# Attention's probabilities turned by VectorE in 32x32 squares instead of by TensorE

## The chip, the cores and the metric

The kernel runs on one core of one Trainium2 chip. TensorE multiplies matrices and can transpose a 128x128 block by a product with an identity matrix, writing to PSUM. VectorE, ScalarE and GpSimd (POOL) work beside it, each with a queue that it works off in order. SyncE (SP) issues the transfers (DMA), also in order. The metric is device time in microseconds, lower is better.

## The reference

A block of a gated cross-attention model on `x` of 8 batches x 512 tokens x 512 columns, all in float32.

```
a  = layernorm(x)
Q, K, V = a @ Wq.T + bq,  ctx @ Wk.T + bk,  ctx @ Wv.T + bv      # 16 heads of 32
P  = softmax(Q K^T / sqrt(32))                                    # per batch and head, 512 x 512
x  = x + tanh(g_xattn) * ((P V) @ Wo.T + bo)
x  = x + tanh(g_ffn) * mixture_of_experts(layernorm(x))           # 8 experts, top 2, capacity 615
```

## The kernel before, in words

The first half of the kernel is attention, the second the experts; the change lies in the first alone.

Attention is cut into 128 **units** (b, c, qc): a batch, a group of four heads (`QH` = 4) and a block of 128 queries. The main loop runs over them in that order, so four units share a (b, c) pair and sixteen a batch. The order of every engine's instructions is the order in which the Python code emits them (`tc.manual_schedule()`); buffers of the pools (`bufs`) and semaphores decide when each can start.

What happens to one unit:

- `scores(u)`: four products of 32 rows (one per head) put 128 queries x 512 keys per head into two PSUM tiles of two banks (`ps_s`, four banks, one unit at a time). VectorE takes the negative row maxima (`nm`, L349, two instructions).
- `soften(u)`: ScalarE takes four exponentials (L356), one per head, into `pr`, and adds up each row (`sums`).
- `turn_heads(u, heads, evict)`: the weights have to be turned, because the product with V sums over keys and so needs keys in the partitions. `turned` (L235) makes four TensorE transposes per head, sixteen per unit, into the ring `ps_t` (two banks). Heads 0 and 1 are copied out by ScalarE (`on_act`, L407), heads 2 and 3 by VectorE (`on_dve`, L410), to `p_t`, one tile per head for the four query blocks of a (b, c) pair.
- `weighted(b, c)`: once the fourth unit of a pair is turned, sixteen products (four key blocks x four heads, 512 columns, L388) give the weighted values `po`. VectorE takes the reciprocals of the sums, POOL spreads them to 32 columns per head (`wide`).
- `divide(b, c, ...)`: four TensorE transposes (L401) turn the reciprocals into `pt_r`, ScalarE copies them (`over`, L403) and VectorE multiplies into `o_t` (L404).

One iteration n of the loop emits, in this order: loads for later (`loads`, SP), the scores of unit n+1, small work on layer norms and the router (`pre`), the weighted values of the last pair if n starts a new one, the turning of heads 0 and 1 of unit n, the exponentials of unit n+1, one projection (`main`: q, k, v or o in turn, L299), `divide`, further small work (`more`: layer norm rows turned on TensorE, router products L276, `add_bo` on POOL), and the turning of heads 2 and 3 of unit n.

A float32 product counts as two matrix instructions in the profile, a transpose as one. Lines in the profile: L251 and L268 copy turned layer norm rows, L218 to L228 are the layer norm on VectorE, L319 and L328 take the v and o projections out of PSUM, L308 and L313 the q and k projections.

The experts' stage already uses the two steps that the change brings into attention: `lay_in` and `lay_out` (L810, L841) move 32-row quarters of a tile inside SBUF by transfers, and `turn_laid` and `lay_out` (L820, L833) transpose 32x32 squares on VectorE.

Of the kernel before, what the change touches and what calls it, by code (L numbers as in the profile page):

```python
# [17 lines left out]
P = 128  # L18
# [3 lines left out]
DC = D // P  # L22
# [22 lines left out]
def gated_block(ctx: ExitStack, tc: tile.TileContext, a: dict, out: bass.AP):  # L45
# [125 lines left out]


    with ExitStack() as at:
        wts = at.enter_context(tc.tile_pool(name="wts", bufs=1))
# [3 lines left out]
        ps_s = at.enter_context(tc.tile_pool(name="ps_s", bufs=2, space=PSUM))  # L178
        ps_t = at.enter_context(tc.tile_pool(name="ps_t", bufs=2, space=PSUM))
        ps_p = at.enter_context(tc.tile_pool(name="ps_p", bufs=1, space=PSUM))  # L180
        ps_o = at.enter_context(tc.tile_pool(name="ps_o", bufs=1, space=PSUM))

# [87 lines left out]
        def route(b):  # L270

            xt = rows_n.pop((3, b))
            pl = ps_o.tile([P, S], F32, tag="po", name="pl")[:, :P]
            for c in range(DC):
                for j in range(TT):
                    nc.tensor.matmul(  # L276
                        pl[j * HD : (j + 1) * HD, :],
                        lhsT=wr[:, c, :],
                        rhs=xt[:, c, j, :],
                        start=(c == 0),  # L280
                        stop=(c == DC - 1),
                    )
            lt = small.tile([P, P], F32, name="lt", bufs=1)
            nc.scalar.activation(lt, pl, AF.Identity, bias=br_c)
            rows_n[4, b] = lt

        def route_turn(b):
            pl = ps_o.tile([P, S], F32, tag="po", name="pl_t")[:, :P]
            nc.tensor.transpose(pl, rows_n.pop((4, b)), ident)
            nc.vector.tensor_copy(  # L290
                logits[:, b * TT : (b + 1) * TT, :], pl.rearrange("p (j e) -> p j e", j=TT)[:, :, :E]
            )
# [12 lines left out]
        def proj_q(b, c, ps=None):  # L305
            ps = group(lambda ic: w["q"][:, ic, cols(c)], lambda ic: xn_t[b][:, ic, :], ps)
            q_t[b, c] = acts.tile([P, S], F32, tag="q_t", name="q_t")
            nc.scalar.activation(q_t[b, c], ps, AF.Identity, bias=bq[:, c : c + 1], scale=SCALE)  # L308

        def proj_k(b, c, ps=None):  # L310
            ps = group(lambda ic: w["k"][:, ic, cols(c)], lambda ic: ctx_t[b][:, ic, :], ps)
            k_t[b, c] = acts.tile([P, S], F32, tag="k_t", name="k_t")
            nc.scalar.activation(k_t[b, c], ps, AF.Identity, bias=bk[:, c : c + 1])  # L313

# [14 lines left out]

        p_sb, p_t, sums, recips = {}, {}, {}, {}  # L330

# [20 lines left out]
        def soften(u, ps, nm):  # L352
            b, c, qc = u
            pr = probs.tile([P, QH, S], F32, tag="pr", name="pr")
            for i in range(QH):
                nc.scalar.activation(  # L356
                    pr[:, i, :],
                    ps[i // 2][:, i % 2, :],
                    AF.Exp,
                    bias=nm[:, i : i + 1],  # L360
                    accum_out=sums[b, c][:, qc, i : i + 1],
                )
            p_sb[u] = pr

        def turn_heads(u, heads, evict):
            b, c, qc = u
            if qc == 0 and heads[0] == 0:
                p_t[b, c] = [
                    probs.tile([P, TT, S], F32, tag=f"p_t{i}", name=f"p_t{i}", bufs=1) for i in range(QH)
                ]  # L370
            for i in heads:
                pt = turned(p_sb[u][:, i, :])
                evict(p_t[b, c][i][:, :, cols(qc)], pt)

        def weighted(b, c):

            if c == 0:
                o_t[b] = acts.tile([P, DC, S], F32, tag="o_t", name=f"o_t{b}")
            rc = small.tile([P, TT, QH], F32, name="rc", bufs=2)
            nc.vector.reciprocal(rc, sums.pop((b, c)))  # L380
            wide = small.tile([P, TT, QH, HD], F32, name="wide", bufs=1)
            nc.gpsimd.tensor_copy(wide, rc.unsqueeze(3).to_broadcast([P, TT, QH, HD]))
            po = ps_o.tile([P, S], F32, tag="po", name="po")
            pts = p_t.pop((b, c))
            for kc in range(TT):
                for i in range(QH):
                    h = QH * c + i
                    nc.tensor.matmul(  # L388
                        po[i * HD : (i + 1) * HD, :],
                        lhsT=v_s[b][:, kc, h * HD : (h + 1) * HD],  # L390
                        rhs=pts[i][:, kc, :],
                        start=(kc == 0),
                        stop=(kc == TT - 1),
                    )
            return po, wide

        def divide(b, c, po, wide):

            pt = ps_t.tile([P, TT, P], F32, tag="pt", name="pt_r")
            for qc in range(TT):  # L400
                nc.tensor.transpose(pt[:, qc, :], wide[:, qc, :, :].rearrange("p h d -> p (h d)"), ident)  # L401
            over = probs.tile([P, S], F32, tag="over", name="over", bufs=1)
            nc.scalar.copy(over, pt.rearrange("p c q -> p (c q)"))  # L403
            nc.vector.tensor_tensor(o_t[b][:, c, :], po, over, ALU.mult)  # L404

        def on_act(dst, src):
            nc.scalar.copy(dst, src)  # L407

        def on_dve(dst, src):
            nc.vector.tensor_copy(dst, src)  # L410

# [42 lines left out]
        for j, t in enumerate((2, 3, 6, 7)):  # L454
            put_ln2(B - 2, (11, 13, 14, 15), B - 1, j, t)

        def loads(b, c, qc):
            if qc == 2 and c == 2 and b + 2 < B:
                load_ctx(b + 2)
            if qc == 0:  # L460
# [7 lines left out]
                if c == DC - 1:  # L468
                    load_x(b, 0, 2)
                    if b == B - 2:  # L470
                        load_x(b, 1, 2)
                elif b == B - 1 and c == 0:
# [5 lines left out]
        with tc.manual_schedule():  # L478
# [44 lines left out]
            nc.gpsimd.tensor_scalar(bo_b, bo_b, tg_x, None, ALU.mult)  # L523
            for n, u in enumerate(units):
                b, c, qc = u
                loads(b, c, qc)
                nxt = units[n + 1] if n + 1 < len(units) else None
                if nxt:
                    ps, nm = scores(nxt)
                for f, *args in pre.pop(n, ()):  # L530
                    f(*args)
                if n and qc == 0:
                    out_of = units[n - 1][:2]
                    po_wide = weighted(*out_of)
                turn_heads(u, (0, 1), on_act)
                if nxt:
                    soften(nxt, ps, nm)
                for f, *args in main.pop(n, ()):
                    f(*args)
                if n and qc == 0:  # L540
                    divide(*out_of, *po_wide)
                for f, *args in more.pop(n, ()):
                    f(*args)
                turn_heads(u, (2, 3), on_dve)
                p_sb.pop(u)

            last = B - 1
            for j in range(1, TT):
                load_x(last, j, 2)
            for j in range(TT):  # L550
                add_bo(last, j)
            divide(last, DC - 1, *weighted(last, DC - 1))
            choose_largest(small, last - 1, 0)
            choose_largest(small, last - 1, 1)
            choose_gates(last - 1)
            assert not pre and not main and not more
# [680 lines left out]
```

## Time and profile before

| | us |
|---|---|
| median of 3 runs | 2106.46 (2105.45 to 2106.7) |
| the profiled execution, its own time | 2106.64 |
| its span, first to last instruction | 2104.5 |

Of the span TensorE's matmuls are busy 95%, its weight loads 59%, VectorE 62%, ScalarE 40%, POOL 29%. Attention runs from the first loads to about 1050 us, the choice of tokens for the experts to about 1120 us, the experts from there to the end.

How the rows are read: the page gives the span in 40 slices, with a digit for the tenths of each slice in which an engine is busy, and a digit for the clock granted to TensorE. A row of windows gives busy microseconds of each engine in one stretch, with instruction counts in brackets. A row of groups names line, engine, operation, tile written and tiles read, shapes and count; then busy time, the mean of one in ns, and the engine's idle time just before, with what ended it.

### The profile page before, as it was taken

What the parts mean: (1) busy time and instruction counts of PE and PEld (TensorE: products, weight loads), DVE (VectorE), ACT (ScalarE), POOL (GpSimd) and SP (SyncE); (2) the same over time, 40 slices, a digit from 0 to 9 for tenths busy, and PEclk for the clock granted to TensorE, in tenths of its full rate; (3) what the DMA queues carried; (4) which work ended last, traced back from release to release, by engine and by line L of the source; (5) the groups of instructions that cost most, each with busy time, mean ns of one, the idle gap of its engine ahead of it and who ended that gap; (6) DMA issues with size and microseconds to landing.
All of it is one profiled execution on the core that took longest, in us unless ns stands there. A gap on an engine that the chain in (4) does not pass through costs nothing.

```text
span 2104.5 us, 27762 instructions
## 1 busy us (share of the span) xinstructions
PE 1994.6 (95%) x9808; PEld 1238.7 (59%) x9808; DVE 1297.9 (62%) x2694; ACT 836.1 (40%) x2014; POOL 604.6 (29%) x800
## 2 busy tenths in 40 slices
PE   8999999999999999999848999999999999999997
PEld 3445555555555555555426676777777777777775
DVE  4566566566665666656566768676767767663540
ACT  3556555555555555555502214041322304032231
POOL 1001101001100101010014374564536455464533
PEclk9999999999999999999969999999999999999998
DMA  6010111102010110100042244544453444535331
GB/s 220 1 56 16 51 41 45 41 21 69 28 56 31 31 65 21 32 31 36 26 122 66 70 117 96 148 110 130 96 134 87 108 120 106 151 84 139 92 74 25
DMA packets 216938, 157.46 MB, mean 75 GB/s; under 512 B 17568, under 2 KB 186208, under 8 KB 216800
## 3 DMA queue, kind: packets, MB, share of 16 engines
q1 hardware_dynamic: 207968, 134.81, 22.1%
q0 software_dynamic: 8832, 20.88, 5.3%
q8 instruction: 78, 1.28, 0.2%
q14 instruction: 60, 0.49, 0.1%
HBM read 107.75 MB, written 29.77 MB: 65 GB/s over the span
## 4 chain that ended last, share of the span: by engine, by line
PE 81%; DVE 6%; ACT 5%; issue 3%; DMA 2%; SPq 2%; POOL 0%; POOLq 0%; ACTq 0%; DVEq 0%
PE ps L900 36%; PE pj L299 20%; PE pt L235 11%; PE s L340 7%; PE po L388 5%; DMA w<-in_W 2%; SPq L841 1%; DVE ht L884 1%; ACT q_t L308 1%; ACT xn_t L268 1%; ACT xn_t L251 1%; ACT over L403 1%; PE pj_o L299 1%; DVE mask L667 1%; ACT h L924 1%
## 5 line engine op out<-in xcount | busy, mean ns | idle before, releaser
L356 ACT ACTIVATE pr<-s,nm 128x512 f32<-128x512 f32 x512 | 347.1, 704 | 2.5 <-DVE nm L349 2.5
L235 PEld LDWEIGHTS pt<-ident,pr 128*128 128x128 f32 x2048 | 224.8, 141 | 175.0 <-DVE p_t L410 76.6
L235 PE MATMUL pt<-ident,pr 128*128 128x128 f32 x2048 | 293.0, 279 | 34.1 <-ACT over L403 13.9
L349 DVE TENSOR_REDUCE nm<-s 128x2 f32<-128x1024 f32 x256 | 301.4, 1218 | 38.2 <-PE s L340 37.4
L407 ACT COPY p_t<-pt 128x512 f32<-128x512 f32 x256 | 137.5, 589 | 408.1 <-PE pt L235 408.1
L222 POOL TENSOR_TENSOR rstd<-rstd,nhalf 128x1 f32<-128x1 f32 x64 | 37.2, 582 | 688.6 <-DVE rstd L221 688.6
L900 PE MATMUL ps<-xg_t,w 128*128 128x308 f32 x768 | 220.1, 423 | 0.5 <-ACT u L953 0.5
L410 DVE COPY p_t<-pt 128x512 f32<-128x512 f32 x256 | 169.7, 686 | 70.6 <-PE pt L235 68.3
L900 PE MATMUL ps<-h,w 128*128 128x308 f32 x768 | 207.5, 425 | 0.0
L900 PEld LDWEIGHTS ps<-xg_t,w 128*128 128x128 f32 x768 | 145.8, 190 | 53.9 <-ACT u L953 1.0
L900 PEld LDWEIGHTS ps<-h,w 128*128 128x128 f32 x768 | 143.7, 190 | 52.6 <-issue 3.1
L340 PE MATMUL s<-k_t,q_t 32*128 32x512 f32 x1024 | 152.2, 646 | 2.9 <-ACT pr L356 2.0
L900 PE MATMUL ps<-tg,s1w 128*128 128x308 f32 x512 | 145.4, 426 | 9.3 <-ACT p1s L928 9.3
L404 DVE TENSOR_TENSOR o_t<-po,over 128x512 f32<-128x512 f32 x32 | 22.1, 691 | 191.6 <-ACT over L403 191.6
L900 PE MATMUL ps<-ht,s2w 128*128 128x308 f32 x512 | 137.9, 426 | 0.0
L924 ACT ACTIVATE h<-c,b 128x308 f32<-128x308 f32 x192 | 101.2, 549 | 74.4 <-DVE c L963 72.7
L900 PEld LDWEIGHTS ps<-tg,s1w 128*128 128x128 f32 x512 | 94.9, 190 | 53.0 <-issue 20.4
L299 PE MATMUL pj<-ctx_t,wk 128*128 128x512 f32 x256 | 117.3, 602 | 7.0 <-DMA ctx_t<-in_ctx_t 7.0
L388 PE MATMUL po<-p_t,v_s 128*32 128x512 f32 x1024 | 119.4, 599 | 0.0
L900 PEld LDWEIGHTS ps<-ht,s2w 128*128 128x128 f32 x512 | 95.5, 190 | 34.8 <-issue 1.8
L356 ACT ACTIVATION_READ_ACCUMULATOR pr<-s,nm 128x1 f32 x512 | 113.9, 222 | 0.0
L299 PE MATMUL pj<-xn_t,wq 128*128 128x512 f32 x248 | 111.6, 592 | 0.0
(192 smaller groups left out, 2960.9 us busy)
## 6 DMA issues: line engine op xcount, KB each, us to landing
w<-in_W SPq DMA_DIRECT2D x128, 256.0 KB, 3.3
w<-in_W SPq DMA_DIRECT2D x64, 512.0 KB, 3.8
x<-in_x SPq DMA_DIRECT2D x64, 256.0 KB, 4.3
laid<-xg SPq DMA_DIRECT2D x140, 64.0 KB, 2.6
out_x<-x SPq DMA_DIRECT2D x32, 256.0 KB, 2.0
xn_rows<-xn SPq DMA_DIRECT2D x32, 256.0 KB, 2.0
ctx_t<-in_ctx_t SPq DMA_DIRECT2D x7, 1024.0 KB
eo<-laid SPq DMA_DIRECT2D x112, 64.0 KB, 2.1
```

Of the source, the lines that this page charges most:

```text
L222: nc.gpsimd.tensor_tensor(rstd, rstd, nhalf, ALU.pow)
L235: nc.tensor.transpose(pt[:, c, :], src[:, c * P : (c + 1) * P], ident)
L299: nc.tensor.matmul(ps, lhsT=lhs(ic), rhs=rhs(ic), start=(ic == 0), stop=(ic == DC - 1))
L340: nc.tensor.matmul(ps[i // 2][:, i % 2, :], lhsT=q_t[b, c][r, cols(qc)], rhs=k_t[b, c][r, :], start=True, stop=True,)
L349: nc.vector.tensor_reduce(nm[:, 2 * i : 2 * i + 2], ps[i], AX.X, ALU.max, negate=True)
L356: nc.scalar.activation(pr[:, i, :], ps[i // 2][:, i % 2, :], AF.Exp, bias=nm[:, i : i + 1], accum_out=sums[b, c][:, qc, i : i + 1],)
L388: nc.tensor.matmul(po[i * HD : (i + 1) * HD, :], lhsT=v_s[b][:, kc, h * HD : (h + 1) * HD], rhs=pts[i][:, kc, :], start=(kc == 0), stop=(k ...
L404: nc.vector.tensor_tensor(o_t[b][:, c, :], po, over, ALU.mult)
L407: nc.scalar.copy(dst, src)
L410: nc.vector.tensor_copy(dst, src)
L900: nc.tensor.matmul(ps, lhsT=lhs[k], rhs=rhs[k], start=(k == 0 and not onto), stop=(k == n - 1), skip_group_check=onto,)
L924: nc.scalar.activation(hh[q, i], src, AF.Silu, bias=b1[:, j : j + 1])
```

## The change

The weights of a unit are no longer turned on TensorE. A 128x128 transpose is split into two steps: rows are moved so that 32x32 squares stand where they must, and VectorE transposes the squares.

- `soften` writes `pr` with the keys in four groups (`[P, DC, QH, P]`) and then issues four transfers on SP, one per group: group g of all 128 rows (256 KB) goes to partitions 32g to 32g+31 of a new tile `laid_p`, four rows of `pr` behind one another in each partition.
- `turn_heads` is now one VectorE square transpose per head, 128x512, from `laid_p` to `p_t`; the ScalarE and VectorE copies out of PSUM are gone.
- So that this comes out in the right order, the q projection stores its columns and the k projection its keys in a permuted order, and the copy `over` undoes the order of the queries (strided access patterns on ScalarE).
- `weighted` now runs per unit, sixteen products of 128 columns instead of sixteen of 512 per pair, two units after the unit's scores block: iteration n emits heads 0 and 1 of unit n-1 turned, scores of n+1, the weighted values of unit n-2, exponentials and transfers of n+1, and heads 2 and 3 of unit n-1. The loop has two more iterations.
- `over_sums` holds the reciprocals and `wide`, after the pair's fourth unit; `divide` follows in the same iteration, now the second of the next pair.
- PSUM: the ring `ps_t` has one bank instead of two, `ps_o` two instead of one; the router's results use `ps_t`.
- Loads: the context of batch b+2 comes in four transfers instead of one; the last batch's x is loaded at its last head group and `add_bo` for it runs in its last four iterations; the choice of the last but one batch (`choose_largest`, `choose_gates`) stands before the last weighted values.

```diff
-        ps_t = at.enter_context(tc.tile_pool(name="ps_t", bufs=2, space=PSUM))
+        ps_t = at.enter_context(tc.tile_pool(name="ps_t", bufs=1, space=PSUM))
-        ps_o = at.enter_context(tc.tile_pool(name="ps_o", bufs=1, space=PSUM))
+        ps_o = at.enter_context(tc.tile_pool(name="ps_o", bufs=2, space=PSUM))
...
-            nc.scalar.activation(q_t[b, c], ps, AF.Identity, bias=bq[:, c : c + 1], scale=SCALE)
+            nc.scalar.activation(
+                q_t[b, c].rearrange("p (t j q) -> p t q j", t=TT, q=DC),
+                ps.rearrange("p (t q j) -> p t q j", t=TT, q=DC),
+                AF.Identity, bias=bq[:, c : c + 1], scale=SCALE,
+            )
...
-            nc.scalar.activation(k_t[b, c], ps, AF.Identity, bias=bk[:, c : c + 1])
+            nc.scalar.activation(
+                k_t[b, c].rearrange("p (g c i) -> p c g i", g=DC, c=DC),
+                ps.rearrange("p (c g i) -> p c g i", g=DC, c=DC),
+                AF.Identity, bias=bk[:, c : c + 1],
+            )
...
         def soften(u, ps, nm):
             b, c, qc = u
-            pr = probs.tile([P, QH, S], F32, tag="pr", name="pr")
+            pr = probs.tile([P, DC, QH, P], F32, tag="pr", name="pr")
             for i in range(QH):
                 nc.scalar.activation(
-                    pr[:, i, :],
-                    ps[i // 2][:, i % 2, :],
+                    pr[:, :, i, :],
+                    ps[i // 2][:, i % 2, :].rearrange("p (g k) -> p g k", g=DC),
                     AF.Exp,
...
+            laid_p[u] = probs.tile([P, DC, QH, P], F32, tag="laid_p", name="laid_p")
+            for g in range(DC):
+                nc.sync.dma_start(
+                    out=laid_p[u][g * BL : (g + 1) * BL].rearrange("p q h k -> p (q h k)"),
+                    in_=pr[:, g].rearrange("p h k -> p (h k)"),
+                )
...
-            for i in heads:
-                pt = turned(p_sb[u][:, i, :])
-                evict(p_t[b, c][i][:, :, cols(qc)], pt)
+        def turn_heads(u, heads):
+            if heads[0] == 0:
+                p_t[u] = probs.tile([P, QH, TT, P], F32, tag="p_t", name="p_t")
+            for i in heads:
+                nc.vector.transpose(
+                    p_t[u][:, i].rearrange("p c (q j) -> p q c j", q=DC),
+                    laid_p[u][:, :, i].rearrange("p q (c i) -> p q c i", c=DC),
+                )
+
+        def weighted(u):
+            b, c, qc = u
+            if qc == 0:
+                values[b, c] = ps_o.tile([P, S], F32, tag="po", name="po")
+            pt = p_t.pop(u)
+            for kc in range(TT):
+                for i in range(QH):
+                    h = QH * c + i
+                    nc.tensor.matmul(
+                        values[b, c][i * HD : (i + 1) * HD, cols(qc)],
+                        lhsT=v_s[b][:, kc, h * HD : (h + 1) * HD],
+                        rhs=pt[:, i, kc, :],
+                        start=(kc == 0),
+                        stop=(kc == TT - 1),
+                    )
...
-            nc.scalar.copy(over, pt.rearrange("p c q -> p (c q)"))
-            nc.vector.tensor_tensor(o_t[b][:, c, :], po, over, ALU.mult)
+            nc.scalar.copy(
+                over.rearrange("p (t q j) -> p t q j", t=TT, q=DC),
+                pt.rearrange("p t (j q) -> p t q j", q=DC),
+            )
+            nc.vector.tensor_tensor(o_t[b][:, c, :], values.pop((b, c)), over, ALU.mult)
...
+        for j in range(TT):
+            put(more, B - 1, 12 + j, add_bo, B - 1, j)
...
-            for n, u in enumerate(units):
-                b, c, qc = u
-                loads(b, c, qc)
+            for n in range(len(units) + 2):
+                if n < len(units):
+                    loads(*units[n])
+                done = units[n - 1] if 0 < n <= len(units) else None
+                if done:
+                    turn_heads(done, (0, 1))
                 nxt = units[n + 1] if n + 1 < len(units) else None
                 if nxt:
                     ps, nm = scores(nxt)
                 for f, *args in pre.pop(n, ()):
                     f(*args)
-                if n and qc == 0:
-                    out_of = units[n - 1][:2]
-                    po_wide = weighted(*out_of)
-                turn_heads(u, (0, 1), on_act)
+                of = units[n - 2] if n > 1 else None
+                if of:
+                    weighted(of)
+                    if of[2] == TT - 1:
+                        wide = over_sums(*of[:2])
                 if nxt:
                     soften(nxt, ps, nm)
+                if done:
+                    turn_heads(done, (2, 3))
+                    laid_p.pop(done)
+                if n == len(units):
+                    choose_largest(small, last - 1, 0)
+                    choose_largest(small, last - 1, 1)
+                    choose_gates(last - 1)
                 for f, *args in main.pop(n, ()):
                     f(*args)
-                if n and qc == 0:
-                    divide(*out_of, *po_wide)
+                if of and of[2] == TT - 1:
+                    divide(*of[:2], wide)
                 for f, *args in more.pop(n, ()):
                     f(*args)
-                turn_heads(u, (2, 3), on_dve)
```

## The prediction

> **What bounds the kernel now.** I read the page's slices first (TensorE 9 tenths busy throughout, attention to about 1050 us), then the windows of the steady stretch 100 to 1000 us, then its groups, the instructions of the two transposing lines that stand after attention, and the last slices by window. TensorE's busy time, two of the windows, columns as wall, PE, PEld, DVE, ACT, POOL, granted clock, DMA share, GB/s:
> ```profile
> 500.00:600.00 100.00, 97.32 (x568) 51.89 (x569) 61.77 (x93) 54.72 (x139) 7.65 (x11) 1.00 0.08 27
> 600.00:700.00 100.00, 97.66 (x556) 51.44 (x554) 64.52 (x106) 57.32 (x144) 10.87 (x15) 1.00 0.15 48
> 1000.00:1050.00 50.00, 41.33 (x290) 22.74 (x290) 29.73 (x53) 28.62 (x75) 2.22 (x3) 0.97 0.08 23
> 1050.00:1100.00 50.00, 23.64 (x104) 11.74 (x97) 30.86 (x134) 4.91 (x9) 6.89 (x9) 0.73 0.45 132
> ```
> TensorE is 97% busy at clock 1.00, VectorE 62%, ScalarE 56%, transfers idle. The groups of 100 to 1000 us (busy us, mean ns, idle before):
> ```profile
> L349 DVE TENSOR_REDUCE nm<-s 128x2 f32<-128x1024 f32 x224 | 263.5, 1218 | 24.9 <-PE s L340 24.6
> L235 PE MATMUL pt<-ident,pr 128*128 128x128 f32 x1792 | 256.0, 279 | 24.0 <-ACT over L403 10.7 <-ACT xn_t L268 6.2 <-ACT xn_t L251 6.0
> L410 DVE COPY p_t<-pt 128x512 f32<-128x512 f32 x224 | 148.7, 686 | 58.1 <-PE pt L235 55.9
> L407 ACT COPY p_t<-pt 128x512 f32<-128x512 f32 x226 | 121.4, 589 | 365.4 <-PE pt L235 365.4
> L388 PE MATMUL po<-p_t,v_s 128*32 128x512 f32 x896 | 102.9, 595 | 0.0
> L276 PE MATMUL pl<-xn_t,wr 128*32 128x128 f32 x192 | 6.5, 276 | 0.0
> ```
> 224 reductions, two per unit, make 112 units: 8.04 us a unit. The evictions wait for TensorE; nothing hides the transposes. The new operation, by its two shapes in the expert stage, and the issue of a transfer of the new kind (L810), with what such transfers took between 1331 and 1341 us (packets, MB, share of 16 engines):
> ```profile
> L833 DVE STREAM_TRANSPOSE laid<-o_t x28: 697/700/706, 1251.5 to 1997.2; 128x512 f32<-128x512 f32 x28
> L820 DVE STREAM_TRANSPOSE xg_t<-laid x28: 1058/1096/1118, 1224.4 to 1951.7; 128x512 f32<-128x512 f32 x28
> L810 SPq DMA_DIRECT2D laid<-xg x140: 547/600/1304, 1215.0 to 1950.5; - x140
> ...
> q1 hardware_dynamic: 1752, 0.80, 29.7%
> ```
> 700 ns where both sides run in blocks of 32 floats, 1096 where the source steps by four.
>
> **The change, per unit of steady attention.** Busy time is summed over the nine windows from 100 to 1000 and divided by 112.
>
> TensorE: 874.9/112 = 7.81 us. The 16 transposes go: 256.0/112 = 2.29. The weighted values become four times 16 products of 128 columns; L388 costs 102.9/28 = 3.68 for four units, the routing (L276, same shape and number) 6.5/6 = 1.08 per 16 products, so 4.33: +0.16 a unit. New 5.7.
>
> VectorE: 560.5/112 = 5.00. Two evictions go, 148.7/112 = 1.33; four square transposes come. I take 0.70 each (L833: the new source and destination also run in blocks of 32), bounds 0.63 (two starts of L833 to the next instruction) and 1.10. 2.80 in: 6.48. VectorE becomes the longest engine.
>
> ScalarE: 507.1/112 = 4.53, less 121.4/112 = 1.08: 3.4. The turned stores of q, k and the sums cost between nothing (the same turned read at L874 took 566 ns) and the 0.39 by which L820 is above L833; I take nothing, as even +0.4 is covered by 3 us of idle ScalarE.
>
> SP and transfers: four issues at 0.60 = 2.4 us of SP a unit, ahead of the loads of x and of the context (now four issues instead of one). 1.05 MB a unit. The expert stage's quarters moved 0.80 MB in 29.7% of the 16 engines' 10 us (last line above), 269 GB/s, which gives 3.9 us; the first loads reached 373 GB/s, 2.8 us; for the other end I halve 269, 7.8 us, since no row shows quarters of 256 KB. I take 3.9, the same pattern. Other transfers are 0.12 x 8 = 1.0 us. 4.9 of 16 engines' time per unit is hidden by two units' delay, as follows.
>
> The added wait: the first square transpose of a unit waits for four transfers, and behind it in VectorE's queue stand the next score maxima, on which exponentials and the next scores hang. From the end of a unit's maxima: exponentials 1.9, issue 2.4, landing 2.1 after the last issue (the 64 KB rows; 5.3 was the median of the quarters laid out beside weight loads), the 3.9 of transfer overlapping the issue: 1.9 + 3.9 + 2.1 = 7.9. VectorE comes to these squares one maxima later: 6.8 for the unit, 0.5 of layer norm and 1.4 for the older unit's last two squares, 8.7. It holds by 0.8 us, so I cost this wait at nothing; if it fails, the squares, the maxima behind them and the next scores are late by the difference. The other buffers are no closer: pr, laid_p and p_t have two each, and a quarter overwrites laid_p only after squares of two units before, which VectorE runs while the exponentials run. The loads of x and of the context stand in SP's queue behind a unit's quarters and ahead of the next unit's, with most of a unit to drain; each takes 0.45 us of SP and the context 3.5 us of transfer (1.05 MB at the same rate or better), once in sixteen units.
>
> Crossing waits: in every fourth unit VectorE ends on the division, which needs scores 1.07, weighted 1.08, k projection 3.6, transposes 0.6, ScalarE copy 0.6, so 7 us from the start of the scores, plus handovers; VectorE is free after 1.2 + 2.35 + 0.54 + 0.24 + 1.4 = 5.7, or 6.7 when the statistics of a tile stand between: about 1 us, 0.25 a unit. What it is ahead or behind by at that moment moves this between 0 and 1.5. Four semaphores at 21 to 50 ns, 0.1. The single bank for turned tiles makes TensorE wait 0.6 for a copy at two or three places of a batch; covered by TensorE's 1.1 us of slack per unit, and worth 0.1 if that is gone. Steady unit: 6.48 + 0.35 = 6.83. Clock: TensorE would be 83% busy; in the 1000 to 1050 row, equally busy, 0.97 was granted, 5.9 us, still covered.
>
> In the first and last batch one LN tile and one projection in four are missing: L218, L219, L221, L228 and L328 sum to 2.31, 0.58 a unit: 6.25. Today nm starts at 38.09 (unit 1) and 1039.39 (unit 127): 1001.3 us for 126 units. New: 96 x 6.83 + 30 x 6.25 = 843. Gain 158.
>
> The tail: now the last exponential ends 1045.0 and the last division 1057.7, 12.7 us, 4.9 of them a wait for x that the moved loads and add_bo (POOL, 1.27 each, idle there) take out. New: landing 6, transposes 2.8, fourteen small instructions of the choice moved in front (0.22 each, 3.1), reciprocal to division 3.3 (0.24, wide 0.62, transposes 0.93, over 0.59, product 0.69 and handovers): 15.2. Loss 3, rounded up. The start: the last early transfer drains before 40 us, the first quarters land behind it, and VectorE wants them at 40.5, after the maxima: 0, at worst 2.
>
> Sum against the profiled execution, 2106.64 us (span 2104.5): 2106.6 - 158 + 3 = 1952. That execution is 0.2 above the median of 2106.46, so 1951.
>
> [...]
> [...]
>
> **Rivals.**
> Late quarters (faster, but less): if the landing after the last issue is 5.3 to 6.8 us (median and longest of the eo quarters) and transfers queue behind context and x, the round over two units is 1.9 + 2.4 + 6.8 + 1.4 + 2.35 = 14.9, 7.4 a unit: 126 x 7.4 = 932, gain 69, 2106.5 - 69 + 3 = 2040. For: 256 KB instead of 64. Against: no weight loads run in attention.
> Transfers as the bound (slower): at 135 GB/s 7.8 + 1.0 = 8.8 a unit, 126 x 8.8 = 1109, +108 + 3: 2217. It decides from about 150 GB/s (1.05 MB in 8 - 1 us). Against: 512-byte packets already make 269.
> Slow squares (slower): at 1.10 VectorE is 8.08 + 0.35 = 8.43, light units 7.85: 96 x 8.43 + 30 x 7.85 = 1045, +44 + 3: 2153. It turns at about 1.0 a square. Against: the blocks of 32.
> No effect: if TensorE's waits merely move to other operations, 2106; nothing in the rows speaks for it, since TensorE keeps 5.7 of 8.04.
>
> **How the numbers follow.** Forecast 62%, own range 1915 to 1995: squares at 0.63 make 6.55 and 5.97 a unit, 808, gain 193, 1916; doubled crossing waits make 7.18 and 6.60, 887, gain 114, 1995. Late quarters 22%. Transfers as the bound 7%, slow squares 6%, no effect 3%. Faster 85%, within 0.2% (what a measurement can tell, 4 us) 2%, slower 13%. The range, 1915 to 2045, runs from the forecast's low end to just over the time of late quarters; outside it stand the three last cases (16%) and a few per cent of the first two.
>
> **What would show it.** Right: transposes of pr gone from TensorE; p_t squares at 0.70; VectorE about 95% busy, TensorE 83%, units 6.5 to 7; little idle before the squares from laid_p. Wrong: idle of several us in front of the squares released by transfers (late quarters, or the bound if the DMA share stands above 0.9), squares near 1.1, a granted clock well under 0.97, or SP waiting on its own earlier transfers, as it does for up to 2.4 us in the first 30 us now. What would make the number wrong without the mechanism: a square transpose dearer than L833's, or crossing waits that repeat in every unit instead of every fourth.

## The result, and the profile after

The changed kernel takes 2226.6 us (median of four runs, 2225.3 to 2231.2) against 2106.6 us for the kernel before on the same chip: a ratio of 1.057, with a 95% interval of 1.054 to 1.059. It is slower by 120 us. The forecast was 1951, faster; the second rival, the transfers as the bound, had said 2217. The profiled execution of the changed kernel has a span of 2225.4 us.

The windows of the steady stretch come first (columns: wall, then busy time of PE, PEld, DVE, ACT and POOL, granted clock, DMA share, GB/s); this is the kernel after:
```profile
300.00:400.00 100.00, 87.46 (x634) 40.92 (x633) 68.51 (x108) 40.50 (x107) 8.74 (x12) 0.88 1.01 150
600.00:700.00 100.00, 83.41 (x593) 38.54 (x594) 72.02 (x125) 42.72 (x112) 9.83 (x14) 0.90 1.00 149
```
Where the kernel before had a DMA share of 0.08 and 0.15, the 16 DMA engines are now busy all the time, while TensorE has fallen from 97% to 83 to 87%, and VectorE, which was to be the longest engine, is at 70%. No compute engine is the bound any more. A share of 1.0 at only 150 GB/s is the line to stop at: at a share of 1.05 the first loads of the kernel before moved 373 GB/s (between 10 and 20 us), and those of the kernel after 367 at 1.04.

The groups of the kernel after between 200 and 900 us (busy us, mean ns, idle time before, and what ended it):
```profile
L389 DVE STREAM_TRANSPOSE p_t<-laid_p 128x512 f32<-128x512 f32 x317 | 204.8, 684 | 170.0 <-DMA laid_p<-pr 163.8 <-issue 5.4 <-PE s L355 0.8
L364 DVE TENSOR_REDUCE nm<-s 128x2 f32<-128x1024 f32 x158 | 183.0, 1196 | 0.0
L403 PE MATMUL po<-p_t,v_s 128*32 128x128 f32 x2560 | 105.4, 316 | 0.0
L312 ACT ACTIVATE q_t<-pj,bq 128x512 f32<-128x512 f32 x20 | 23.8, 1189 | 7.0 <-PE pj L303 7.0
```
158 maxima, two per unit, are 79 units in 700 us: 8.86 us a unit in this stretch, where the kernel before needed 8.04. The square transposes cost 684 ns, as forecast. What is wrong stands behind the second bar: VectorE is idle 170 us ahead of them, and transfers end 163.8 us of that. In the kernel before VectorE was idle ahead of its evictions too, but TensorE ended that wait (55.9 of 58.1 us between 100 and 1000), and TensorE itself was 97% busy.

The chain that ended last, followed through one round of two units of the kernel after (start us, length us, what):
```profile
612.81 1.31 DVE p_t L389 x2
614.12 2.24 DVE nm L364 x2
...
617.98 1.17 DVE p_t L389 x2
...
619.20 0.56 SPq L380
619.81 0.59 SPq L380
620.45 0.60 SPq L380
621.10 10.83 DMA laid_p<-pr
...
632.05 1.30 DVE p_t L389 x2
```
From the last of a unit's issues to the first square transpose that may run, 10.8 us pass; the prediction had 2.1. VectorE's next maxima stand behind those squares, so the next exponentials start late as well (ScalarE waits 351.7 us of the 700 between 200 and 900 for maxima). The next transfers are released by squares too: the tile that they write is free only after the two older squares behind the maxima (617.98 us and 1.17 more), and the last exponential had ended at 618.0. Between 200 and 900 us squares come last before SP's first issue 79 times, once in every unit.

The bytes and time of SP's queue over the whole span, kernel after (packets, MB, share of 16 engines):
```profile
q1 hardware_dynamic: 281984, 269.07, 66.9%
```
The same line of the kernel without these transfers (the second run of "No transfers" below) is:
```profile
q1 hardware_dynamic: 208256, 134.82, 23.9%
```
66.9% of 2225.4 is 1488.8 us of all 16 engines, 23.9% of 1933.9 is 462.2. The difference, 1027 us, is what the 134.2 MB of quarters took (128 units of 1.05 MB): 8.0 us a unit, 131 GB/s. With the 1.0 us of other transfers that is, to within 2%, the whole of the unit's 8.86. The rates below are all found in this way.

The 120 us add up along the score maxima. Their lines in the kernel before, the kernel after and the kernel without these transfers (duration in ns, then first and last start in us):
```profile
L349 DVE TENSOR_REDUCE nm<-s x256: 1210/1215/1226, 30.0 to 1040.7; 128x2 f32<-128x1024 f32 x128
```
```profile
L364 DVE TENSOR_REDUCE nm<-s x256: 1182/1206/1225, 33.1 to 1155.1; 128x2 f32<-128x1024 f32 x128
```
```profile
L364 DVE TENSOR_REDUCE nm<-s x256: 1179/1205/1225, 32.6 to 871.4; 128x2 f32<-128x1024 f32 x128
```
From before to after the start gives 3, the units 111, and what follows the last maxima, 1070.3 against 1063.8, the remaining 6.

### The profile page after: what moved, and what is told of

It is laid out like the page before. It is cut to its first block, busy times and chain, and to the rows that moved or that the text cites. A ratio compares the mean times of both kernels' runs of the same rounds, so it can differ in the third digit from the quotient of the medians.

```text
span 2225.4 us, 31078 instructions
## 1 busy us (share of the span) xinstructions
PE 1960.4 (88%) x10832; PEld 1158.9 (52%) x10832; DVE 1432.9 (64%) x2950; ACT 721.1 (32%) x1758; POOL 604.7 (27%) x800
## 3 DMA queue, kind: packets, MB, share of 16 engines
q1 hardware_dynamic: 281984, 269.07, 66.9%
## 4 chain that ended last, share of the span: by engine, by line
PE 38%; DMA 29%; DVE 17%; SPq 6%; ACT 5%; issue 3%; POOL 0%; DVEq 0%; POOLq 0%; ACTq 0%
PE ps L923 36%; DMA laid_p<-pr 27%; DVE p_t L389 6%; DVE nm L364 5%; SPq L380 5%; ACT pr L371 3%; DMA w<-in_W 1%; SPq L864 1%; DVE ht L907 1%; DVE bnst L222 1%; DVE mask L690 0%; PE idle L1127 0%; DVE xn L232 0%; DMA wv<-in_Wv_t 0%; PE s_o L303 0%
## 5 line engine op out<-in xcount | busy, mean ns | idle before, releaser
L389 DVE STREAM_TRANSPOSE p_t<-laid_p 128x512 f32<-128x512 f32 x512 | 330.6, 684 | 290.8 <-DMA laid_p<-pr 270.2
L355 PE MATMUL s<-k_t,q_t 32*128 32x512 f32 x1024 | 255.1, 775 | 93.4 <-ACT pr L371 91.7
L403 PEld LDWEIGHTS po<-p_t,v_s 128*32 128x32 f32 x4096 | 131.2, 129 | 144.7 <-issue 124.5
L403 PE MATMUL po<-p_t,v_s 128*32 128x128 f32 x4096 | 180.6, 325 | 11.3 <-DVE p_t L389 11.3
L355 PEld LDWEIGHTS s<-k_t,q_t 32*128 32x128 f32 x1024 | 69.5, 213 | 198.3 <-ACT pr L371 179.6
L303 PE MATMUL pj<-ctx_t,wk 128*128 128x512 f32 x256 | 133.5, 669 | 6.8 <-DMA ctx_t<-in_ctx_t 6.8
L303 PE MATMUL pj<-xn_t,wq 128*128 128x512 f32 x248 | 124.4, 647 | 0.0
L303 PE MATMUL pj<-wv,ctx_t 128*128 128x512 f32 x240 | 114.4, 620 | 0.0
L303 PE MATMUL pj<-wo,o_t 128*128 128x512 f32 x232 | 109.2, 614 | 0.0
L371 ACT ACTIVATION_READ_ACCUMULATOR pr<-s,nm 128x1 f32 x512 | 103.7, 203 | 0.0
```

The costliest lines, as they stand in the source:

```text
L303: nc.tensor.matmul(ps, lhsT=lhs(ic), rhs=rhs(ic), start=(ic == 0), stop=(ic == DC - 1))
L355: nc.tensor.matmul(ps[i // 2][:, i % 2, :], lhsT=q_t[b, c][r, cols(qc)], rhs=k_t[b, c][r, :], start=True, stop=True,)
L371: nc.scalar.activation(pr[:, :, i, :], ps[i // 2][:, i % 2, :].rearrange("p (g k) -> p g k", g=DC), AF.Exp, bias=nm[:, i : i + 1], accum_o ...
L389: nc.vector.transpose(p_t[u][:, i].rearrange("p c (q j) -> p q c j", q=DC), laid_p[u][:, :, i].rearrange("p q (c i) -> p q c i", c=DC),)
L403: nc.tensor.matmul(values[b, c][i * HD : (i + 1) * HD, cols(qc)], lhsT=v_s[b][:, kc, h * HD : (h + 1) * HD], rhs=pt[:, i, kc, :], start=(k ...
```

## The experiments

Theory one after the result: the transfers are the bound because each ends in 32 neighbouring partitions. Rivals: any copy inside SBUF runs at this rate; reading, not writing, is slow; a transfer of few partitions is slow wherever they lie; the wait costs, not the rate; or something else in the change holds the units long. The diffs are against the kernel after where nothing else is said. A unit's time is from here on the mean over all units: from the first start of the maxima to the last, less 1.2 us for the last unit's own first half, over 127. That is 7.95 us in the kernel before and 8.83 in the kernel after.

### No transfers

```diff
-            pr = probs.tile([P, DC, QH, P], F32, tag="pr", name="pr")
+            pr = probs.tile([P, DC, QH, P], F32, tag="pr", name="pr", bufs=4)
...
-            laid_p[u] = probs.tile([P, DC, QH, P], F32, tag="laid_p", name="laid_p")
-            for g in range(DC):
-                nc.sync.dma_start(...)
+            laid_p[u] = pr
```


> The transfers inside SBUF are left out: VectorE transposes the squares straight from pr (four buffers instead of two of pr and two of laid_p), so the weights reach the products with wrongly placed quarters; all other work is as in the changed kernel. Theory (the transfers set the pace, 8.8 us a unit): without them a unit takes 6.5 to 7.0 us and the kernel 1930 to 1990 us, VectorE 90% busy or more in attention. Rival (the crossing waits, the strided store of q at 1.19 us and the lower granted clock set the pace, the transfers only fill the time): it stays above 2100 us.

Measured: 2135.3 us, which can't be read against the others, since the chip granted TensorE a clock of at most 0.85 in this run (0.836 on average), in the experts' stage too, where the others had 1.00. Even so a unit took 7.07 us. It was run again with repeats.

> The first run without the transfers was granted a clock of 0.84 for its whole length, in the experts' stage too, so its time can't be set beside the others. The same kernel again, timed against the kernel before: the four transfers of a unit are left out, the squares are turned straight from the exponentials' tile (four of these), so the attention's weights are not those of the reference. Theory (the transfers cost the time, and nothing else in the change does): VectorE bounds a unit at about 6.8 us as in the run with the spread transfers (1941), 1920 to 1960, granted clock 0.96 or more. Rival (something in the change other than the transfers keeps a low clock or long units): above 2050 again.

Measured: 1936.8 us (1934.6 to 1941.3), a ratio of 0.920 to the kernel before (0.917 to 0.922). The windows' line of the steady stretch:
```profile
200.00:770.00 570.00, 547.46 (x4552) 263.96 (x4551) 522.09 (x875) 317.09 (x807) 67.82 (x93) 1.00 0.15 51
```
A unit takes 6.60 us (the 6.8 and 6.83 in expectations count the maxima between 200 and 900 us, but here the last one starts at 871.4); in the steady stretch VectorE is 92% busy, TensorE 96%. All of the rest of the change together is worth 170 us, where 155 were forecast; the transfers take 290 back.

### The same bytes, other partitions

Spread over 128 partitions:
```diff
-                    out=laid_p[u][g * BL : (g + 1) * BL].rearrange("p q h k -> p (q h k)"),
+                    out=laid_p[u][:, g].rearrange("p h k -> p (h k)"),
```


> The four transfers of a unit carry the same bytes in the same 2 KB runs, 128 per transfer, but each goes from 128 partitions to the same 128 partitions, so the quarters are not laid out (the weights reach the products wrongly placed). Theory A (a transfer that ends in 32 partitions is slow): the transfers fall from 7.8 us a unit to 3.9 or less, VectorE sets the pace, 1930 to 2000 us. Theory B (any copy from SBUF to SBUF runs at about 130 GB/s, since SBUF is read and written): nothing changes, 2200 to 2240 us, transfer engines at 1.0.

Every fourth partition:
```diff
-                    out=laid_p[u][g * BL : (g + 1) * BL].rearrange("p q h k -> p (q h k)"),
+                    out=laid_p[u][g::DC].rearrange("p q h k -> p (q h k)"),
```


> As the changed kernel, but transfer g of a unit ends in every fourth partition (g, g+4, ... g+124) instead of 32 neighbouring ones: the same 32 partitions per transfer, the same 2 KB runs and 8 KB per partition, but over the whole height of SBUF (rows wrongly placed for the squares). [...] If what counts is that only 32 partitions take 8 KB each, or theory B: 2200 to 2240 us.

Reading 32 neighbours, writing all 128:
```diff
-                    out=laid_p[u][g * BL : (g + 1) * BL].rearrange("p q h k -> p (q h k)"),
-                    in_=pr[:, g].rearrange("p h k -> p (h k)"),
+                    out=laid_p[u][:, g].rearrange("p h k -> p (h k)"),
+                    in_=pr[g * BL : (g + 1) * BL].rearrange("p q h k -> p (q h k)"),
```


> The transfer turned round: each reads 32 neighbouring partitions (8 KB each) and writes all 128 (2 KB each); the quarters are not laid out. If only the writing end is narrow (theory A): 1930 to 2000 us. If a narrow reading end costs as much: 2200 to 2240 us, as theory B also says. Between the two: the reading end costs something less than the writing end.

Measured (one run each): 1941.4, 1938.9 and 2007.8 us. SP's queue in the three, in this order, each from its own page:
```profile
q1 hardware_dynamic: 281984, 269.07, 42.2%
```
```profile
q1 hardware_dynamic: 281984, 269.07, 42.4%
```
```profile
q1 hardware_dynamic: 281984, 269.07, 53.5%
```
By the same subtraction: 356 us or 377 GB/s, 359 us or 374 GB/s, and 611 us or 220 GB/s. Packets and bytes are those of the kernel after. The comparison of the second run with it is the sharpest: with every fourth partition each transfer still ends in 32 partitions with 8 KB in each, and only which 32 has changed; the rate goes from 131 to 374. So neither the copy inside SBUF nor the number of partitions is the cause. Reading 32 neighbours is dear too, but less, between the two times expected: the transfers take 4.8 us a unit, the unit 7.09, and the squares wait for transfers 45 us of the 700 between 200 and 900 in the trace, in place of 164. The wait by itself is no rival either: in the first two runs the squares still have to wait for their transfers, which now land sooner, a unit takes 6.60 us, and the times are 2 to 5 us above the run without transfers, less than the 7 us by which that run's own repeats differ.

### Which neighbours

Four changes of the same transfers: the order of issue 0, 2, 1, 3; quarters 2 and 3 from ScalarE's queue; two transfers into 64 neighbours each; and every second partition of one half.
```diff
-            for g in range(DC):
+            for g in (0, 2, 1, 3):
```


> The kernel after, with the four quarters of a unit issued in the order 0, 2, 1, 3, so that neighbouring transfers end in partitions 0 to 31, 64 to 95, 32 to 63 and 96 to 127. Theory A (each transfer by itself is limited by its 32 neighbouring partitions and the next one in the queue waits behind it, packet by packet): no change, 2215 to 2240. Theory B (the limit is shared by the two quarters of one half of the partitions, and transfers in different halves run side by side): units of 7 to 8 us, 1980 to 2130.


```diff
-                nc.sync.dma_start(
+                (nc.sync if g < 2 else nc.scalar).dma_start(
```


> The kernel after, with quarters 0 and 1 of a unit issued by SP and quarters 2 and 3 by ScalarE, in another queue, so that the two halves of the partitions are written from two queues at once. Theory A (the 16 engines themselves are held up by writes into 32 neighbouring partitions, whichever queue they come from): DMA share near 1.0 and 8.5 to 9 us a unit again, 2200 to 2260, or a little more for the issues that now stand among the exponentials. Theory B (each queue goes through its packets in order and only one quarter's partitions are written at a time; two queues in two halves double the rate): about 260 GB/s, units near 7 us, 1940 to 2010.


```diff
-            for g in range(DC):
+            for g in range(2):
                 nc.sync.dma_start(
-                    out=laid_p[u][g * BL : (g + 1) * BL].rearrange("p q h k -> p (q h k)"),
-                    in_=pr[:, g].rearrange("p h k -> p (h k)"),
+                    out=laid_p[u][g * 2 * BL : (g + 1) * 2 * BL].rearrange("p q h k -> p (q h k)"),
+                    in_=pr[:, 2 * g : 2 * g + 2].rearrange("p g h k -> p (g h k)"),
```


> The kernel after with two transfers of 512 KB a unit in place of four of 256 KB, the first ending in partitions 0 to 63, the second in 64 to 127, 16 KB in each; bytes, runs and wait as before. The weights then lie in the wrong partitions, so the values are not those of the reference. [...] Theory B (what counts is the number of partitions that a transfer ends in): about 260 GB/s, 4 + 1 us a unit, 1940 to 2000.


```diff
-                    out=laid_p[u][g * BL : (g + 1) * BL].rearrange("p q h k -> p (q h k)"),
+                    out=laid_p[u][g // 2 * 64 + g % 2 : g // 2 * 64 + 64 : 2].rearrange("p q h k -> p (q h k)"),
```


> The kernel after with each quarter ending in every second partition of one half (0, 2, ... 62, then 1, 3, ... 63, and the same from 64 on) in place of 32 neighbours; values not those of the reference. Every fourth of all 128 ran at 372 GB/s, 32 neighbours at 131. [...] Theory B (neighbouring partitions disturb one another, two of a group of four as little as one): 1940 to 2000. [...]

Measured (one run each):

| transfers end in | issued | us | unit, us | rate of the quarters, GB/s |
|---|---|---|---|---|
| 32 neighbours (the kernel after) | SP, 0 1 2 3 | 2226.6 | 8.83 | 131 |
| 32 neighbours | SP, 0 2 1 3 | 2237.4 | 8.86 | 131 |
| 32 neighbours | SP 0 1, ScalarE 2 3 | 2196.2 | 8.57 | 139 |
| 64 neighbours | SP, two | 2292.8 | 9.32 | 124 |
| every second of 64 | SP, 0 1 2 3 | 2204.7 | 8.68 | 135 |
| every fourth of 128 | SP, 0 1 2 3 | 1938.9 | 6.60 | 374 |

SP's queue with the order 0, 2, 1, 3, with 64 neighbours and with every second partition, each from its own page:
```profile
q1 hardware_dynamic: 281984, 269.07, 66.5%
```
```profile
q1 hardware_dynamic: 245120, 269.05, 67.5%
```
```profile
q1 hardware_dynamic: 281984, 269.07, 66.0%
```
Twice the partitions in the same half bring nothing (124 GB/s against 131); that kernel is even slower than the kernel after, where the theory that the number of partitions counts had 1940 to 2000, and why is not known. Leaving gaps in the half brings 3% (135 against 131). In these runs the 374 GB/s come only where a single transfer reaches both halves; the five others of the table have 124 to 139. Two transfers issued together, one into each half and from two queues, gain 6% (139 against 131); SP's and ScalarE's queues in that run, from its page:
```profile
q1 hardware_dynamic: 245120, 201.94, 42.8%
q10 hardware_dynamic: 36864, 67.13, 22.3%
```
The moved half of the bytes brings its time along, 22.3% of 2194.4 for 67 MB, and the engines are as full as before: the DMA share is 0.99 between 200 and 900 us. How the 16 engines share out one transfer, and why a second one in the other half does not fill the gaps of the first, no record here shows. Nor does any run show why transfers into 32 neighbours get 131 GB/s, about a third of the 374, or why reading 32 neighbours costs less than writing them (220 against 131).

### Shorter runs

```diff
-            pr = probs.tile([P, DC, QH, P], F32, tag="pr", name="pr")
+            pr = probs.tile([P, QH, DC, P], F32, tag="pr", name="pr")
...
-                    out=laid_p[u][g * BL : (g + 1) * BL].rearrange("p q h k -> p (q h k)"),
-                    in_=pr[:, g].rearrange("p h k -> p (h k)"),
+                    out=laid_p[u][g * BL : (g + 1) * BL].rearrange("p q h k -> p (q h) k"),
+                    in_=pr[:, :, g],
```


> The kernel after, with the same quarters into the same 32 neighbouring partitions, in runs of 512 bytes in place of 2 KB: the shape of the row of 269 GB/s that the prediction took its 3.9 us from. Theory A (that row misled since quarters of 64 KB, one by one, with little else in flight, do not show what a steady stream into 32 partitions gets): 131 GB/s or less again, 8 us or more a unit, 2215 to 2450. Theory B (the run length is what made the difference, 512-byte runs being spread over the 16 engines otherwise than 2 KB runs): 200 to 269 GB/s, 5 to 6.3 us a unit with the other transfers, 1940 to 2010.

Measured (one run): 2339.0 us, 9.68 us a unit. The line of the steady stretch, and SP's queue from the page:
```profile
200.00:900.00 700.00, 567.22 (x3855) 262.78 (x3856) 445.12 (x723) 265.25 (x683) 55.47 (x77) 0.87 1.17 142
```
```profile
q1 hardware_dynamic: 478592, 269.07, 77.0%
```
The share is above 1, so the times of packets overlap on an engine and the rate can only be bounded: 100 GB/s by the shares, 121 by the unit less 1.0 us of other transfers. Both are under 131, so the prediction's 269, read from packets of 512 bytes, is not what packets of 512 bytes do in a full queue. In the prediction's row a packet took 0.297 x 10 us x 16 / 1752 = 27 ns; here, with 262144 of them in 1337 us of 16 engines, 82 ns.

### The squares first

If only the partitions at the far end are wrong, the order of the two steps can be turned round: VectorE turns the squares straight from the exponentials, and the transfers lay the turned blocks out afterwards. They then read 32 neighbours and write all 128, and what waits for them is TensorE, two units later. The weighted values need every key in its own partition, in any order, so k is stored in the order that the transfers leave (key t x 128 + i x 4 + c of the c-th square goes to partition 4i + c), and q and the sums are in their plain order again.
```diff
-                k_t[b, c].rearrange("p (g c i) -> p c g i", g=DC, c=DC),
-                ps.rearrange("p (c g i) -> p c g i", g=DC, c=DC),
+                k_t[b, c].rearrange("p (c t i) -> p c t i", c=DC, t=TT),
+                ps.rearrange("p (t i c) -> p c t i", c=DC, t=TT),
...
+                nc.vector.transpose(
+                    laid_p[u][:, :, i],
+                    p_sb[u][:, i, :].rearrange("p (c t i) -> p c t i", c=DC, t=TT),
+                )
+            if heads[-1] == QH - 1:
+                p_sb.pop(u)
+                sq = laid_p.pop(u)
+                p_t[u] = probs.tile([P, DC, QH, TT, BL], F32, tag="p_t", name="p_t")
+                for g in range(DC):
+                    nc.sync.dma_start(
+                        out=p_t[u][:, g].rearrange("p h t j -> p (h t j)"),
+                        in_=sq[g * BL : (g + 1) * BL].rearrange("p c h t j -> p (c h t j)"),
+                    )
...
-                        rhs=pt[:, i, kc, :],
+                        rhs=pt[:, :, i, kc, :],
...
-                done = units[n - 1] if 0 < n <= len(units) else None
+                done = units[n] if n < len(units) else None
```


> A version with the whole computation of the reference: VectorE turns the squares first, straight from the exponentials' tile, and only then four transfers lay the turned blocks out, each reading 32 neighbouring partitions and ending in all 128 (a key's place among the partitions is 4i+c, and k is stored in that order). The transfers then have the rate of the run that reads 32 neighbours, 219 GB/s: 4.8 + 1.0 us a unit beside VectorE's 6.5 to 6.8, and no engine's queue but TensorE's waits for them, two units later. Theory (only the rate into 32 neighbouring partitions made the change slow): VectorE's 6.8 us a unit are the bound, 1930 to 1970, faster than both kernels. Rival (a steady stream of transfers also slows the engines' own reads and writes, or the transfers come too late for the weighted values): 1990 to 2060, with TensorE waiting for p_t.

Measured: 2000.1 us (1993.6 to 2002.0), 0.948 of the kernel before (0.946 to 0.951): faster than both kernels, but not at the 1930 to 1970 expected; it lies in the range of the rival (1990 to 2060, with TensorE waiting for `p_t`). The rate is 224 GB/s, near the 219 expected, and a unit takes 7.05 us. Lines from the table of waits of this kernel between 200 and 900 us (us in total, times, longest):
```profile
DVE laid_p L378 <- DMA p_t<-laid_p: 40.1, 46, 1.9
DVE o_t L425 <- ACT over L424: 28.7, 24, 1.4
PE po L401 <- DMA p_t<-laid_p: 19.7, 21, 2.0
PEld po L401 <- DMA p_t<-laid_p: 15.1, 15, 2.0
```
VectorE still waits for transfers, now before it may overwrite a block of two units ago; TensorE waits for blocks that are not there yet. So all four squares of a unit were moved ahead of the next maxima (diff against this version):
```diff
                 if done:
-                    turn_heads(done, (0, 1))
+                    turn_heads(done, range(QH))
...
-                if done:
-                    turn_heads(done, (2, 3))
```


> The version with the squares first, with all four squares of a unit turned together ahead of the next maxima, so that the four transfers start some 3.5 us earlier; whole computation. In the version before it VectorE waited 40 us and TensorE 35 us of 700 for the turned blocks' transfers (a buffer not yet read out, a block not yet landed), and a unit took 7.07 us in place of 6.83. Theory (those waits are all that the slower transfers cost): they go, 6.8 to 6.9 us a unit, 1935 to 1965. Rival (the 0.8 of DMA share itself delays other work, such as x and the context, or the transfers' rate falls where they start earlier): 1980 to 2005 again. Second rival (maxima now stand behind squares that wait for the exponentials of the unit, which is a new wait): 2000 to 2060.

Measured: 1993.1 us (1989.9 to 1996.2), 0.945 of the kernel before (0.942 to 0.948); 7.01 us a unit. The waits of the same stretch:
```profile
PEld s L349 <- ACT pr L365: 65.8, 90, 2.7
DVE o_t L425 <- ACT over L424: 60.2, 25, 2.5
DVE x L337 <- PE pj L303: 22.5, 20, 2.4
PEld po L401 <- DMA p_t<-laid_p: 6.8, 9, 0.8
```
The theory's first half held: the waits for the transfers are nearly gone. Its second half fell: the time came back elsewhere. Without the squares of two heads between the maxima and the division, VectorE comes to the division sooner after its own reciprocal and waits out what lies between the two (POOL's spread, TensorE's transposes, ScalarE's copy; in the timeline the reciprocal starts at 609.39 us and the division at 612.03): 60 us in place of 28.7, and 22.5 for a projection in place of 4.8. The first rival's number, 1980 to 2005, came true, but neither by a lower rate (225 GB/s) nor by other transfers that come late (they end 5.7 us of waits in the 700). What is left against the 1937 of no transfers, 56 us, lies mostly in these waits: the 96 units of the middle six batches take 673.7 us, 38 more than without transfers, and in them the division's wait is 26 us longer (58.3 against 32.0) and that of v's and o's projections 12 (23.2 against 10.8). That moving the squares away from the division caused this is argued from the timeline; putting the division elsewhere was not tried.

## Why the prediction was wrong

**The step that failed** is in the paragraph on SP and transfers: "I take 3.9, the same pattern." The transfers take 8.0 us a unit. The end that is written was the same, 32 neighbours (in packets of 512 bytes there, of 2 KB here); the state of the queue was not. Twelve quarters of 64 KB were issued over 7.8 us, and 0.80 MB in the window's 10 us is 80 GB/s that actually moved. Dividing the bytes by the packets' busy time gave 269, which would be a rate only if a packet took as long when the queue is full; the run with shorter runs shows three times as long (82 ns against 27). The bound that the prediction named for its other end, 7.8 us, came close by luck: it was 269 halved, with no row behind the halving.

**What followed from it.** "It holds by 0.8 us, so I cost this wait at nothing" had the landing 2.1 us after the last issue; it was 8.5 to 11 in the chain between 600 and 660 us. But the wait is not the mis-sized term by itself: with the same dependences and transfers at 374 GB/s the time is 2 to 5 us above that of no transfers. The sentence that the older squares free `laid_p` "while the exponentials run" did not hold either: they ended last before the first issue in every unit, also in the run with spread transfers (102 of 102 between 200 and 900 us), where it cost next to nothing. The rival transfers as the bound had the mechanism and its place, and by the halved rate also its price (8.8 a unit against 8.83; 2217 against 2226.6). "It decides from about 150 GB/s" fits the runs: 139 is still slower than the kernel before (2196.2 us), 220 faster (2007.8). What spoke "Against" it was the same 269. It was given 7%.

**What was right**, shown by the runs without the transfers or with spread ones:
- The time: 1951 forecast, 1937 to 1941 in these runs, inside the forecast's own range of 1915 to 1995.
- Squares at 0.70 each: 679 ns on average, of which 635 count as busy (265.4 us for 418), since the next one starts before the last has ended; the bound of 0.63 was named for that. "Slow squares" never came up.

**What came out right by misses that cancel.** A steady unit was to take 6.83 us; it takes 6.62 (without transfers the maxima of unit 16 start at 137.2 us, those of unit 112 at 772.8). VectorE is busy 6.06 of that, not 6.48, and idle 0.56, not the 0.35 of the crossing waits (in these 96 units 32.0 us for the division's copy, 10.8 for projections and 7.2 for scores). The units of the first and last batch were to be 0.58 shorter; they take about 6.5, shorter by 0.1. Start and tail, 3 in the sum, give 1.3. So over all units 6.60 stands against 843/126 = 6.69, and that the sum lies within 14 us of the time is in part luck.

**What was off and cost little.** TensorE was to have 5.7 us a unit and be 83% busy, with VectorE as the longest engine; without transfers it has 6.36 and 96%, more than VectorE. Per unit of the same 96 the scores go from 1.15 to 1.35, the projections from 3.56 to 3.67 at a clock of 0.99, and the weighted values take 1.10 (1.08 forecast); the rest is that less of their time overlaps. The two engines are nearly level; that small waits in v's or the division's path therefore show at once in the last two kernels is argued, not shown. The turned store of q was bounded by 0.39 and costs 0.50 (1189 ns, 690 before), of k and the sums next to nothing (medians of 697 and 585); without transfers the other engines wait 4.2 us for q's stores in the whole span. The clock, "covered" at the 0.97 of one row of 50 us, was 0.88 to 0.93 in the kernel after in stretches of 100 us between 200 and 1100 us, where TensorE is 83 to 89% busy.

## What to carry to other kernels

Bytes over busy time, taken from a burst that was fed by slow issues, was not the rate of a full queue here; take what moved per microsecond of wall as the lower end and let the range reach there, since the sustained streams were two to nearly three times slower (131 and 100 GB/s against 269). For copies inside SBUF ask first which partitions one transfer touches: 32 neighbours, or 64, ran at 124 to 139 GB/s however they were ordered or queued, the same bytes in every fourth partition at 374. Where a 32-neighbour side can't be avoided, put it on the reading side (220 GB/s here, against 131 on the writing side) and behind the vector work; with all squares of a unit together VectorE's wait for these transfers went from 40.1 us of 700 to none in the table of waits.

## What the runs showed of the hardware that was not expected

- Every fourth of 128 partitions against 32 neighbours: 374 against 131 GB/s with equal bytes, packets and packet size.
- An issue on SP took longer in the runs whose 256 KB transfers read 32 neighbours: a median of 956 ns (reading 32 neighbours, writing 128) and 1108 (squares first), in place of 602, at a DMA share of 0.8, while the kernel after, at 1.0, has 602. The 64 KB quarters of the experts' stage that read 32 neighbours (L841 in the kernel before) have 602 too. Why is open.
- A ScalarE store into SBUF in steps of four floats takes 1189 ns for 128x512, the plain one 690; a store in runs of 32 floats takes 697 at the median.
- One run was granted a clock of at most 0.85, from the first unit to the last expert, 0.836 on average, and took 10% longer; the same program had 0.97 on average in its next runs.
